# Finishing the next image's layer 0 before layer 3, outputs on another queue, and a new order for the last image's gated MLP

## The chip, the cores and the metric

The kernel runs on one core of one Trainium2 chip. The metric is device time in microseconds (us), as the median of several executions. The engines are named as in the profile: PE is TensorE (matrix multiplies), PEld its weight loads, DVE is VectorE, ACT is ScalarE, POOL is GpSimd, SP is SyncE, which here only issues DMAs.

## The reference

Four images of 192 channels by 64 x 64 positions, float32, go through four layers:

- Layer 0: LayerNorm; a 3x3 convolution gives offsets for a deformable gather (nine taps, bilinear); channel attention (six heads) with a projection, and a residual; then LayerNorm, an MLP 192 to 768 to 192 with exact GELU, and a residual.
- Layer 1: non-local attention of all 4096 positions with each other, in 96 channels (theta, phi, g), projected back, and a residual.
- Layer 2: attention in overlapping 8x8 windows, a projection, a gate made of pyramid means and a depthwise 3x3; then a gated MLP:

```python
z = gelu(fc1(layernorm(x)))           # 768 channels
z1, z2 = z[:384], z[384:]
x = x + fc2(z1 * dwconv3x3(layernorm(z2)))
```

- Layer 3: the means of an image's channels go through a small net to four weights per channel; these are the taps of a causal depthwise 3x3 (the row above and the left neighbour), plus a bias: the output.

## The kernel before

**The loop over images.** For each image b: `keys(b)` makes phi and g for all positions, `layer1(b)` runs the attention, with layer 0's gather of image b+1 woven between its steps, `windows(b)` does the window attention, and `rest(b)` does projection and gate, the gated MLP and layer 3. For b = 1 and 2, `offsets(b+1)` (LayerNorm and offset convolution of the image after next) is made chunk by chunk beside the keys. Positions are worked in eight chunks of 512 (NCH = 8).

**Layer 0's MLP of the next image.** `mlp0(b+1)` needs the gather's result only, so `rest(b)` weaves it beside its own work. It is a generator of 33 steps: one of preparation and four for each chunk i, here written i.w01, i.w23, i.w45n1, i.n0. The first three widen two blocks of 128 hidden channels each (matmuls L844 and L851, Gelu on ACT L858); the third also narrows the upper 64 channels (L870), the fourth the lower 128 (L867), adds the result (L874 on DVE), and stores the chunk to DRAM by SP's queue (L894). `keys(b+1)` loads that store again (L907, also SP) ahead of its first matmul (L910); then come g (L915), and the copies of phi by ACT (L911) and of g by DVE (L918). The last step of the last chunk ends with `keep_warm(p, 12)` (L737), matmuls whose results nobody reads.

**Credits.** The projection, the MLP and layer 3 yield amounts; `rest` adds them up, and for each whole credit runs one step of `mlp0`:

```python
for part in main():
    credit += part
    while credit >= 1.0:
        next(other, None)
        credit -= 1.0
for _ in other:
    pass
```

With the amounts before, the last three steps of `mlp0` (7.w23, 7.w45n1, 7.n0 with keep_warm) fall to layer 3's yields. In the last image (`alone`) there is no next one and `other` is empty.

**What sets the order.** Inside the gated MLP the order on each engine is the order of the program, written out by hand (`tc.manual_schedule()`), with the woven steps of `mlp0` in it. Outside it (layer 3, keys, offsets) the framework's planner orders instructions when the kernel is compiled: by readiness in its own estimate of times, ties by program order. Each engine and each DMA queue then runs its own list strictly in order.

**The gated MLP.** It works in four rounds j = 0..3, each on a pair of chunks: `widen(j, ms)` (fc1 for blocks ms, L1574 and L1576, Gelu L1580; blocks 0 to 2 are z1, 3 to 5 are z2), `gate_mean`, `gate_difference`, `gate_square`, `gate_variances`, `gate_scale` (the LayerNorm of z2: L1586, L1590, L1595, L373, L1613), and the depthwise taps of older pairs. A depthwise needs a row of the next pair, so round j does the upper taps of pair j-1 and the lower ones of pair j-2, then `narrow(j-2)` (fc2, L1659 and L1664) and `end()` (L1673, adds to x and sums its channels). After the four rounds a tail does the last two pairs, `pairs - 2` and `pairs - 1`. The taps are DVE multiply-adds (L1377); in the last image two of nine taps (five in the last pair) are matmuls by diagonals on PE (L1368), with DVE joining in at L1370. L1647 multiplies the finished gate into z1. z1, z2 and the accumulators have two buffers each; the MLP's matmuls share five PSUM banks "h".

**Layer 3.** Means (L1766 ff.), the small net (L1771, L1782, L1785), the weights w (L1789); then six units u. ACT writes the first tap (L1819), POOL a column (L1822), DVE adds the three others (L1838), and the unit is stored by one or two DMAs of SP's queue (L1840, L1844). `o` has three buffers. In the last image one unit's taps run on PE.

Of the kernel before, what the change touches and what calls it, by code (L numbers as in the profile page):

```python
# [24 lines left out]
M, Q = 128, 64  # L25
NCH = 8
# [55 lines left out]
def conv_seq_kernel(ctx: ExitStack, tc: tile.TileContext, a, out: bass.AP):  # L82
# [1459 lines left out]
    def mlp(b, x, sums, sb, ps, taps, hn):  # L1542


        with ExitStack() as s:
# [134 lines left out]
            with tc.manual_schedule():  # L1680
                in_order.append(None)
                for j in range(pairs):
                    lo, hi, upper, lower = 2 * j, 2 * j + 1, j - 1, j - 2
                    if lower >= 0:
                        lower_taps(lower, 0)
                    if upper >= 0:
                        yield 1.0
                    widen(j, (3, 4))
                    if lower >= 0:
                        lower_taps(lower, 1)  # L1690
                    yield 1.0
                    if lower >= 0:
                        lower_taps(lower, 2)
                        narrow(lower, (0, 1))
                        narrow(lower, (2,))
                    if upper >= 0:
                        upper_taps(upper, 0, 2)
                    end()
                    widen(j, (5, 0))
                    gate_mean(lo)  # L1700
                    gate_mean(hi)
                    if upper >= 0:
                        upper_taps(upper, 0)
                        upper_taps(upper, 1, 2)
                    gate_difference(lo)
                    gate_square(lo)
                    gate_difference(hi)
                    widen(j, (1,))
                    gate_square(hi)
                    widen(j, (2,))  # L1710
                    if upper >= 0:
                        upper_taps(upper, 1)
                        upper_taps(upper, 2, 2)
                    gate_variances(lo, hi)
                    norm = None
                    if j + 1 < pairs:
                        norm = pair_norm_steps(x, j + 1, sb, ps, f"l2n2_{b}_{j + 1}")
                        links(norm, SQUARE)
                    yield 1.0
                    if norm is not None:  # L1720
                        links(norm, VARIANCE)
                        table(GELU)
                    gate_scale(lo)
                    gate_scale(hi)
                    hns.pop(j)
                    if norm is not None:
                        hns[j + 1] = links(norm)
                    if upper >= 0:
                        upper_taps(upper, 2)
                for m in range(3):  # L1730
                    lower_taps(pairs - 2, m)
                    yield 1.0
                narrow(pairs - 2, (0, 1, 2))
                for m in range(3):
                    upper_taps(pairs - 1, m, 2)
                    end()
                    yield 0.5
                    upper_taps(pairs - 1, m)
                    yield 0.6
                    lower_taps(pairs - 1, m)  # L1740
                    yield 0.7
                narrow(pairs - 1, (0, 1))
                narrow(pairs - 1, (2,))
                end()
                in_order.pop()


    def layer3(b, x, sums, ps, alone):

        with ExitStack() as s:  # L1750
# [37 lines left out]
            w = s1.tile([M, 2, 4], F32, name=f"w3_{b}", tag="w")  # L1788
            nc.vector.tensor_tensor(w, pw, VW["l3_b2"][:, :, 0:4], ALU.add)  # L1789
            flat = out[b].rearrange("c h w -> c (h w)")  # L1790
            diag = None
            if alone:
                diag = s1.tile([M, 4, M], F32, tag="diag3", name=f"diag3_{b}")
# [2 lines left out]
            for u in (0, 1, 2, 4, 3, 5):  # L1796
                k = u // 4
                o = sb.tile([M, UN], F32, tag="o", name=f"out_{b}_{u}", bufs=3)
                ov = o.rearrange("p (r c) -> p r c", c=W)
                bias3 = VW["l3_bias"][:, k]  # L1800
                if alone and u == 1:
                    xv = x[:, 0 : 4 * UN].rearrange("p (r c) -> p r c", c=W)
                    for j in range(0, UR, 8):
                        at = UR * u + j
                        src, up = xv[:, at : at + 8], xv[:, at - 1 : at + 7]
                        p = ps.tile([128, CN], F32, tag="h", name=f"po3_{b}_{u}_{j}")
                        pv = p.rearrange("p (r c) -> p r c", c=W)
                        terms = [
                            (1, pv, up),
                            (0, pv[:, :, 1:W], up[:, :, 0 : W - 1]),  # L1810
                            (2, pv[:, :, 0 : W - 1], up[:, :, 1:W]),
                            (3, pv[:, :, 1:W], src[:, :, 0 : W - 1]),
                        ]
                        for n, (tap, to, of) in enumerate(terms):
                            nc.tensor.matmul(to, lhsT=diag[:, tap, :], rhs=of, start=n == 0, stop=n == 3, skip_group_check=True)
                        nc.scalar.activation(ov[:, j : j + 8], pv, AF.Identity, bias=bias3)
                else:
                    src = x[:, bass.ts(u, UN)].rearrange("p (r c) -> p r c", c=W)
                    nc.scalar.activation(  # L1819
                        ov[:, :, 1:W], src[:, :, 0 : W - 1], AF.Identity, bias=bias3, scale=w[:, k, 3:4]  # L1820
                    )
                    nc.gpsimd.tensor_copy(ov[:, :, 0:1], bias3.unsqueeze(1).to_broadcast([M, UR, 1]))  # L1822
                    if k == 0:

                        a0 = 1 if u == 0 else 0
                        xv = x[:, 0 : 4 * UN].rearrange("p (r c) -> p r c", c=W)
                        rows = [(ov[:, a0:], xv[:, UR * u - 1 + a0 : UR * u + UR - 1])]
                    else:
                        v, two = 2 * (u - 4), o.rearrange("p (k r c) -> p k r c", k=2, c=W)
                        rows = [(two[:, i, 1:8], blocks[:, v + i, 0:7]) for i in range(2)]  # L1830
                        rows.append((two[:, :, 0], over[:, v : v + 2, 0]))
                    for to, up in rows:
                        for tap, to, of in (
                            (1, to, up),
                            (0, to[..., 1:W], up[..., 0 : W - 1]),
                            (2, to[..., 0 : W - 1], up[..., 1:W]),
                        ):
                            nc.vector.scalar_tensor_tensor(to, of, w[:, k, tap : tap + 1], to, ALU.mult, ALU.add)  # L1838
                if k == 0:
                    nc.sync.dma_start(out=flat[0:M, bass.ts(u, UN)], in_=o)  # L1840
                else:
                    to = flat[M:C].rearrange("c (j h n) -> c j h n", h=2, n=CN)[:, 2 * (u - 4) : 2 * (u - 4) + 2]
                    for h in range(2):
                        nc.sync.dma_start(out=to[:, :, h], in_=o[half(h)].rearrange("p (k n) -> p k n", k=2))  # L1844
                yield 0.7

    def rest(b, x, others, oi, sums, m2):


        with ExitStack() as s:  # L1850
            alone = m2 is None
            sb = s.enter_context(pool_of(name="norms", bufs=1))
            ps = s.enter_context(pool_of(name="restps", bufs=2, space=PSUM))
            wide = s.enter_context(pool_of(name="restps2", bufs=5, space=PSUM))
            psums = Psums({"n": ps, "v": ps, "h": wide}, {"t": "h"})
            other = iter(())
            if not alone:
                other = mlp0(b + 1, m2, s.enter_context(pool_of(name="l0d", bufs=1)), sb, psums)
            credit = 0.0

            def main():
                hn = []

                def ahead():
                    hn.append(links(pair_norm_steps(x, 0, sb, psums, f"l2n2_{b}_0")))

                yield from project(b, x, others, oi.pop(), psums, HFT_PE if alone else (), ahead)
                yield from mlp(b, x, sums, sb, psums, GATE_PE if alone else (), hn)
                yield from layer3(b, x, sums, psums, alone)

            for part in main():
# [6 lines that stand above are left out]
# [170 lines left out]
```

## Time and profile before

| what | value |
|---|---|
| median of 3 runs | 6800.64 us (6798.39 to 6806.05) |
| profiled execution | 6757.88 us |
| its span | 6756.1 us |
| mean granted TensorE clock | 0.952 |
| PE busy | 6155.1 us, 91% |
| DVE busy | 4694.1 us, 69% |
| ACT busy | 3599.2 us, 53% |
| POOL busy | 2065.4 us, 31% |
| output stores on SP's queue, images 0 to 2 | 8 per image (4 of 512 KB, 4 of 256 KB) |
| rest of image 0: last product L1647 to first key matmul L910 | 2298.28 to 2335.82 us |
| last image: rounds 1, 2, 3 and tail of the gated MLP | 6482.0, 6532.7, 6601.4, 6658.1 to 6721.0 us |

The page gives the busy time of each engine in one profiled execution, and slices of the span with the busy tenths of each engine and the granted clock of PE. The timeline lists runs of instructions by start, duration, engine, line and operation, with the idle time before them in brackets and what ended it. Windows give busy times for chosen stretches. Timeline and windows share the time axis, microseconds from the start of the span. All rounds of the last image are measured at the steps of DVE: from the first upper taps of one round to those of the next.

### The profile page before, as it was taken

What the parts mean: (1) busy time and instruction counts of PE and PEld (TensorE: products, weight loads), DVE (VectorE), ACT (ScalarE), POOL (GpSimd) and SP (SyncE); (2) the same over time, 40 slices, a digit from 0 to 9 for tenths busy, and PEclk for the clock granted to TensorE, in tenths of its full rate; (3) what the DMA queues carried; (4) which work ended last, traced back from release to release, by engine and by line L of the source; (5) the groups of instructions that cost most, each with busy time, mean ns of one, the idle gap of its engine ahead of it and who ended that gap; (6) DMA issues with size and microseconds to landing.
All of it is one profiled execution on the core that took longest, in us unless ns stands there. A gap on an engine that the chain in (4) does not pass through costs nothing.

```text
span 6756.1 us, 115795 instructions
## 1 busy us (share of the span) xinstructions
PE 6155.1 (91%) x45392; PEld 4180.0 (62%) x45392; DVE 4694.1 (69%) x6908; ACT 3599.2 (53%) x6136; POOL 2065.4 (31%) x2276
## 2 busy tenths in 40 slices
PE   7687999999989899999998899999998889999986
PEld 4455578786644458887654457878664457776532
DVE  3664279985677758996576848988567867765656
ACT  3664368774444358885444338877444435544332
POOL 2654057662200027672210007765220000012200
PEclk8788999999989899999999999999999999999998
DMA  6885156661010156663110047665101010010000
GB/s 188 260 280 177 54 177 217 215 196 42 8 43 15 59 181 200 219 211 93 29 31 26 17 132 218 216 208 165 35 24 30 17 54 10 15 28 22 4 7 21
DMA packets 330496, 699.37 MB, mean 104 GB/s; under 512 B 60077, under 2 KB 217181, under 8 KB 329182
## 3 DMA queue, kind: packets, MB, share of 16 engines
q0 software_dynamic: 92736, 455.22, 21.0%
q1 hardware_dynamic: 236382, 235.95, 12.3%
q8 instruction: 358, 5.87, 0.4%
q14 instruction: 188, 1.54, 0.1%
q10 hardware_dynamic: 832, 0.79, 0.0%
HBM read 611.25 MB, written 78.87 MB: 102 GB/s over the span
## 4 chain that ended last, share of the span: by engine, by line
PE 51%; DVE 17%; ACT 4%; issue 4%; DMA 2%; SPq 0%; POOL 0%; another core or an unknown queue 0%; DVEq 0%; ACTq 0%; POOLq 0%
PE y L1031 8%; PE s L963 7%; PE h L634 3%; PE v L1196 2%; PE h L1574 2%; DVE ha L1377 2%; PE qk L1121 2%; PE qk L1122 2%; PE t L1204 1%; DVE gate L1377 1%; PE zm L1586 1%; DVE ga L1377 1%; PE h L1576 1%; PE s L1157 1%; PE rb L1270 1%
## 5 line engine op out<-in xcount | busy, mean ns | idle before, releaser
L616 POOL DMA_INDIRECT ring<-table,idx x1152 | 1634.7, 1419 | 1132.5 <-issue 217.8
L963 PE MATMUL s<-ths,ph 96*128 96x256 f32 x4096 | 991.5, 383 | 8.5 <-ACT xo L626 2.7
L963 PEld LDWEIGHTS s<-ths,ph 96*128 96x128 f32 x4096 | 784.0, 193 | 137.1 <-ACT ths L957 4.7
L622 ACT ACTIVATE row<-ring,pos 128x384 f32<-128x384 f32 x1152 | 672.0, 608 | 204.3 <-DVE xo L627 111.3
L1031 PE MATMUL y<-sc,gx 128*97 128x256 f32 x3008 | 724.7, 383 | 18.4 <-ACT yn L1037 15.1
L623 DVE SCALAR_TENSOR_TENSOR row<-ring,fr,row 128x384 f32<-128x384 f32 x1152 | 674.8, 613 | 91.6 <-ACT row L622 63.1
L1031 PEld LDWEIGHTS y<-sc,gx 128*97 128x97 f32 x3008 | 492.5, 165 | 150.8 <-ACT yn L1037 16.5
L626 ACT ACTIVATE xo<-row,pos 128x192 f32<-128x192 f32 x1152 | 485.8, 448 | 156.9 <-remote 63.8
L627 DVE SCALAR_TENSOR_TENSOR xo<-row,fr,xo 128x192 f32<-128x192 f32 x1152 | 447.1, 412 | 123.3 <-issue 60.6
L1028 DVE TENSOR_TENSOR sc<-sc,mbs 128x1024 f32<-128x1024 f32 x376 | 453.4, 1218 | 46.1 <-ACT mbs L989 26.5
L965 ACT COPY sc<-s 128x1024 f32<-128x1024 f32 x376 | 377.5, 1004 | 177.5 <-PE s L963 141.5
L970 DVE TENSOR_TENSOR top<-top,sc 128x1024 f32<-128x1024 f32 x282 | 344.5, 1222 | 137.4 <-ACT sc L965 115.9
L634 PE MATMUL h<-ti,xo 128*128 128x192 f32 x2304 | 437.1, 328 | 0.0
L1029 ACT ACTIVATE sc<-sc 128x1024 f32<-128x1024 f32 x376 | 393.4, 1053 | 75.6 <-DVE sc L1028 66.5
L634 PEld LDWEIGHTS h<-ti,xo 128*128 128x128 f32 x2304 | 390.9, 190 | 29.0 <-issue 8.6
L1180 DVE TENSOR_REDUCE es<-ex 128x6 f32<-128x384 f32 x264 | 133.3, 546 | 365.0 <-ACT ex L1176 365.0
L634 PE MATMUL h<-kept,xo 128*128 128x192 f32 x960 | 255.9, 402 | 114.1 <-DVE xo L627 61.5
L634 PEld LDWEIGHTS h<-kept,xo 128*128 128x128 f32 x960 | 183.0, 224 | 209.5 <-DVE xo L627 98.6
L1624 POOL COPY gate<-gate 128x192 f32<-128x192 f32 x12 | 4.2, 351 | 1000.4 <-ACT gate L1617 855.0
L1377 DVE SCALAR_TENSOR_TENSOR ga<-gate,v,ga 128x1024 f32<-128x1024 f32 x234 | 300.4, 1284 | 6.7
L1031 PE MATMUL y<-se,gx 128*97 128x256 f32 x1088 | 268.3, 387 | 8.6 <-ACT se L1029 8.1
L858 ACT ACTIVATE gl<-h,bias_fc 128x256 f32<-128x256 f32 x384 | 151.2, 474 | 232.9 <-PE h L851 232.5
(391 smaller groups left out, 11213.0 us busy)
## 6 DMA issues: line engine op xcount, KB each, us to landing
ti<-table SPq DMA_DIRECT2D x768, 48.0 KB
ring<-table,idx POOLq DMA_INDIRECT x1152
xnd<-xn SPq DMA_DIRECT2D x4, 3270.0 KB
xi<-in_x_dram SPq DMA_DIRECT2D x32, 384.0 KB
xk<-xd SPq DMA_DIRECT2D x32, 384.0 KB
xd<-xc SPq DMA_DIRECT2D x64, 192.0 KB
table<-tt SPq DMA_DIRECT2D x32, 384.0 KB
xc<-xd SPq DMA_DIRECT2D x60, 192.0 KB
```

Of the source, the lines that this page charges most:

```text
L616: nc.gpsimd.indirect_dma_start(out=gt.rearrange("p q r c -> p (q r c)"), out_offset=None, in_=corners, in_offset=bass.IndirectOffsetOnAxis ...
L622: nc.scalar.activation(row, gt[:, 0], AF.Copy, scale=pos[:, t, 9 + tap : 10 + tap])
L623: nc.vector.scalar_tensor_tensor(row, gt[:, 1], fr[:, t, 9 + tap : 10 + tap], row, ALU.mult, ALU.add)
L626: nc.scalar.activation(xo[:, j, :], row[:, 0, :], AF.Copy, scale=pos[:, t, tap : tap + 1])
L627: nc.vector.scalar_tensor_tensor(xo[:, j, :], row[:, 1, :], fr[:, t, tap : tap + 1], xo[:, j, :], ALU.mult, ALU.add)
L634: nc.tensor.matmul(acc[m // 2][:, bass.ts(m % 2, C)], lhsT=xo.rearrange("p j c -> p (j c)")[:, bass.ts(m, 128)], rhs=tt, start=t == 0 and ...
L963: nc.tensor.matmul(p[:, t, :], lhsT=ph[:, bass.ts(G * g + t, 128)], rhs=ths[i], start=True, stop=True)
L965: nc.scalar.copy(to, p)
L1028: nc.vector.tensor_tensor(ex, ex, mbs[i].unsqueeze(1).to_broadcast([128, G, QN]), ALU.add)
L1029: nc.scalar.activation(ex, ex, AF.Exp)
L1031: nc.tensor.matmul(py, lhsT=gx[:, G * g + t, :], rhs=ex[:, t, :], start=g == 0 and t == 0, stop=g == NG - 1 and t == G - 1,)
L1377: nc.vector.scalar_tensor_tensor(acc[:, b], src(tap, b), w[:, tap : tap + 1], acc[:, b], ALU.mult, ALU.add)
```

## The change

There are four edits.

1. In images 0 to 2 the nine yields of the MLP's tail give 0.9 each instead of 0.5, 0.6 and 0.7, and a new `yield 4.0 * NCH` ahead of layer 3 makes room for whatever of `mlp0` is left. Counted out, the tail's nine yields now run 5.n0, 6.w01, 6.w23, 6.w45n1, 6.n0, 7.w01, 7.w23, 7.w45n1 and 7.n0, one each, so that all 33 steps are done and the new yield finds none. Before, six steps (5.n0 to 7.w01) fell to the tail and three to layer 3. 7.n0 with its keep_warm comes into the MLP's hand-written order, ahead of the last `narrow`.
2. Layer 3's eight output DMAs per image are issued by POOL (`nc.gpsimd`) in images 0 to 2; the last image's stay on SP.
3. In the last image (`taps`) a round puts `widen(5, 0)`, the means, the differences and the first square ahead of `narrow(lower)`, `end()` and the upper taps, and one step of upper taps behind the next pair's squares; the tail mixes upper taps of the last pair with lower ones of the one before, and narrows block by block.
4. In images 0 to 2 the two calls `narrow(lower, (0, 1))`, `narrow(lower, (2,))` of a round become `narrow(lower, (0, 1, 2))`: the matmuls of the upper channels (L1664) of blocks 0 and 1 no longer stand ahead of those that read block 2 (L1659).

```diff
@@ gated MLP, a round j
                     if lower >= 0:
                         lower_taps(lower, 2)
-                        narrow(lower, (0, 1))
-                        narrow(lower, (2,))
-                    if upper >= 0:
-                        upper_taps(upper, 0, 2)
-                    end()
-                    widen(j, (5, 0))
-                    gate_mean(lo)
-                    gate_mean(hi)
...
+                    if taps:
+                        widen(j, (5, 0))
+                        gate_mean(lo)
+                        gate_mean(hi)
+                        gate_difference(lo)
+                        gate_square(lo)
+                        gate_difference(hi)
+                        if lower >= 0:
+                            narrow(lower, (0, 1, 2))
+                        end()
+                        widen(j, (1,))
+                        gate_square(hi)
+                        if upper >= 0:
+                            upper_taps(upper, 0, 2)
+                        widen(j, (2,))
+                        gate_variances(lo, hi)
+                        if upper >= 0:
+                            upper_taps(upper, 0)
+                            upper_taps(upper, 1, 2)
+                    else:
+                        if lower >= 0:
+                            narrow(lower, (0, 1, 2))
...
                     yield 1.0
+                    if taps and upper >= 0:
+                        upper_taps(upper, 1)
+                        upper_taps(upper, 2, 2)
@@ gated MLP, the tail
+                one, two = pairs - 2, pairs - 1
+                if taps:
+                    lower_taps(one, 0)
+                    upper_taps(two, 0)
+                    lower_taps(one, 1)
+                    upper_taps(two, 1)
+                    narrow(one, (0,))
+                    lower_taps(one, 2)
+                    narrow(one, (1,))
+                    narrow(one, (2,))
+                    upper_taps(two, 2)
                     end()
-                    yield 0.5
-                    upper_taps(pairs - 1, m)
-                    yield 0.6
-                    lower_taps(pairs - 1, m)
-                    yield 0.7
-                narrow(pairs - 1, (0, 1))
-                narrow(pairs - 1, (2,))
+                    for m in range(3):
+                        lower_taps(two, m)
+                        narrow(two, (m,))
+                else:
...
+                    for m in range(3):
+                        upper_taps(two, m, 2)
+                        end()
+                        yield 0.9
+                        upper_taps(two, m)
+                        yield 0.9
+                        lower_taps(two, m)
+                        yield 0.9
+                    narrow(two, (0, 1))
+                    narrow(two, (2,))
                 end()
@@ layer3
+            by = nc.sync if alone else nc.gpsimd
...
-                    nc.sync.dma_start(out=flat[0:M, bass.ts(u, UN)], in_=o)
+                    by.dma_start(out=flat[0:M, bass.ts(u, UN)], in_=o)
...
-                        nc.sync.dma_start(out=to[:, :, h], in_=o[half(h)].rearrange("p (k n) -> p k n", k=2))
+                        by.dma_start(out=to[:, :, h], in_=o[half(h)].rearrange("p (k n) -> p k n", k=2))
@@ rest
                 yield from mlp(b, x, sums, sb, psums, GATE_PE if alone else (), hn)
+                yield 4.0 * NCH
                 yield from layer3(b, x, sums, psums, alone)
```

More of the change, by code (lines that the diff above doesn't have):

```diff
@@ L1683, in mlp @@
                     lo, hi, upper, lower = 2 * j, 2 * j + 1, j - 1, j - 2
+                    more = j + 1 < pairs
                     if lower >= 0:
@@ L1693, in mlp @@
                         lower_taps(lower, 2)
-                        narrow(lower, (0, 1))
-                        narrow(lower, (2,))
-                    if upper >= 0:
-                        upper_taps(upper, 0, 2)
-                    end()
-                    widen(j, (5, 0))
-                    gate_mean(lo)
-                    gate_mean(hi)
[L1702 to L1714, printed above, removed]
+                    if taps:
[20 more added lines that the diff above has]
+                            narrow(lower, (0, 1, 2))
+                        if upper >= 0:
+                            upper_taps(upper, 0, 2)
+                        end()
+                        widen(j, (5, 0))
+                        gate_mean(lo)
+                        gate_mean(hi)
+                        if upper >= 0:
+                            upper_taps(upper, 0)
+                            upper_taps(upper, 1, 2)
+                        gate_difference(lo)
+                        gate_square(lo)
+                        gate_difference(hi)
+                        widen(j, (1,))
+                        gate_square(hi)
+                        widen(j, (2,))
+                        if upper >= 0:
+                            upper_taps(upper, 1)
+                            upper_taps(upper, 2, 2)
+                        gate_variances(lo, hi)
@@ L1715, in mlp @@
                     norm = None
-                    if j + 1 < pairs:
+                    if more:
                         norm = pair_norm_steps(x, j + 1, sb, ps, f"l2n2_{b}_{j + 1}")
@@ L1719, in mlp @@
                     yield 1.0
-                    if norm is not None:
+                    if taps and upper >= 0:
+                        upper_taps(upper, 1)
+                        upper_taps(upper, 2, 2)
+                    if more:
                         links(norm, VARIANCE)
@@ L1725, in mlp @@
                     hns.pop(j)
-                    if norm is not None:
+                    if more:
                         hns[j + 1] = links(norm)
@@ L1729, in mlp @@
                         upper_taps(upper, 2)
[L1730 to L1735, printed above, removed]
-                    end()
-                    yield 0.5
-                    upper_taps(pairs - 1, m)
-                    yield 0.6
-                    lower_taps(pairs - 1, m)
-                    yield 0.7
-                narrow(pairs - 1, (0, 1))
-                narrow(pairs - 1, (2,))
+                one, two = pairs - 2, pairs - 1
[9 more added lines that the diff above has]
+                    upper_taps(two, 2)
+                    end()
+                    for m in range(3):
[3 more added lines that the diff above has]
+                    for m in range(3):
+                        lower_taps(one, m)
+                        yield 1.0
+                    narrow(one, (0, 1, 2))
+                    for m in range(3):
+                        upper_taps(two, m, 2)
+                        end()
+                        yield 0.9
[5 more added lines that the diff above has]
+                    narrow(two, (2,))
                 end()
```

## The prediction

> **What bounds the kernel now.** I read the page's slices first, then the transition from image 0 to image 1 in the timeline and in windows, then the same for the other images, and last the gated MLP of the last image. TensorE (PE) is busy 91% of the span and its chain holds 51% of it, so time is to be had only where PE idles or runs at a lower clock. The slices show where:
>
> ```profile
> PE   7687999999989899999998899999998889999986
> PEclk8788999999989899999999999999999999999998
> ```
>
> A slice is 169 us. PE is full while keys and scores run, and at 8 or less near the rests (the windows, MLP and layer 3 of an image), and at the very end. All three edits lie there. The timeline of the first transition (start, duration, engine, line, operation; in brackets the idle before and its releaser):
>
> ```profile
> 2298.28 1.28 DVE L1647 SCALAR_TENSOR_TENSOR z<-gate,v,z 128x1024 f32<-128x1024 f32 x1
> 2307.35 0.17 DVE L1789 TENSOR_TENSOR w<-pw,wide 128x8 f32<-128x8 f32 x1 [2.35 <-PE pw L1785]
> 2307.24 3.78 PE L844 MATMUL h<-d_l0m,fc 128*128 128x256 f32 x8
> ...
> 2308.88 9.50 DVE L1838 SCALAR_TENSOR_TENSOR out<-x,w,out 128x960 f32<-128x960 f32 x8 [1.36 <-ACT out L1819]
> ...
> 2316.04 2.81 PE L870 MATMUL o<-gl,fc 128*64 128x256 f32 x24
> ...
> 2318.78 5.42 PE L867 MATMUL o<-gl,fc 128*128 128x512 f32 x12
> ...
> 2325.55 8.01 PE L737 MATMUL o<-bias,ident 128*128 128x384 f32 x24 [1.36 <-DVE xa L874]
> ...
> 2335.82 2.54 PE L910 MATMUL tp<-xk,phiT 96*96 96x512 f32 x4 [2.26 <-DMA xk<-xd]
> ```
>
> Layer 3 can start at w (2307.35). While VectorE (DVE) works it off, PE does what is left of layer 0's MLP of the next image: widen (L844), narrow (L870, L867) and 8 us of keep_warm (L737). The keys follow only at 2335.8, since they read that MLP's output back. Windows by stage (length, busy time of PE, PEld, DVE, ACT, POOL, granted clock, DMA share, GB/s):
>
> ```profile
> 2243.00:2303.50 60.50, 52.63 (x214) 27.24 (x210) 48.73 (x59) 13.65 (x26) 1.92 (x14) 0.94 0.08 24
> 2303.50:2336.00 32.50, 27.63 (x121) 16.85 (x122) 25.30 (x39) 11.44 (x15) 11.62 (x15) 0.89 0.41 127
> 2336.00:2390.00 54.00, 53.46 (x295) 33.42 (x295) 17.89 (x24) 17.70 (x26) 0.00 (x0) 0.84 0.34 96
> ...
> 2340.00:2344.00 4.00, 4.00 (x12) 2.36 (x11) 0.56 (x1) 0.00 (x0) 0.00 (x0) 0.50 0.26 73
> ```
>
> PE idles 7.9 us in the MLP's tail and 4.9 in layer 3, and then the keys run at half clock: the windows of 4 us from 2336 to 2356 have 0.63, 0.50, 0.50, 0.50 and 0.73. That is 4 x (0.37+0.5+0.5+0.5+0.27) = 8.6 us lost, at a full engine. Image 1 has the same (0.84 over 3926 to 3980); image 2 has not, its gap ahead of the keys is 1.46 us.
>
> **Part 1: layer 0's MLP ends ahead of layer 3.** By the credits, the tail's nine yields now give a step each, and the last three steps leave layer 3. Useful PE work moved per image: two widens of two blocks (8 x L844 1.9 + 8 x L851 1.1 = 3.0 each, 6.0), narrow(1) 2.8, narrow(0) 5.4: 14.2 us. With them go 8.0 us of keep_warm, two L874 sums on DVE (0.48 + 0.75), four Gelus each of two widens on ACT (1.57 each four) and three xd stores on SP, which stand nowhere near their limits. The tail has 7.9 us of PE idle, but in bits beside DVE's taps (48.7 of 60.5 us busy), so the last z multiply comes later by between 14.2 - 7.9 - 5.4 = 1 us (narrow(0) stands behind it and delays no tap) and 14.2 - 7.9 = 6.3; I take 4: it ends at 2303.6 instead of 2299.6. Then the hand order bites: inside the MLP PE keeps the order written, so keep_warm (8.0) and what it waits for (L874, 0.75) stand ahead of the last narrow. That takes 3.7 + 1.9 + 2.0 + 1.1 = 8.7 us: 2303.6 + 0.75 + 8.0 + 8.7 = 2321, then end() 1.5, the means and the small net 4, so w comes about 2326, 18 us later than 2307.4. Layer 3's 25 us of DVE end near 2352 instead of 2334.
>
> Against that: the keys' PE need not wait for layer 3. Their input was stored before keep_warm ended, so they start near 2321 instead of 2335.8, 14.8 us earlier, with no gap ahead and so up to 8.6 us of clock. What is late next is DVE: each of the keys' eight chunks needs a gx copy (0.56), and in images 1 and 2 the LayerNorm for offsets 3.45 us more (1.22 + 0.95 + 1.28), while layer 3's multiplies are ahead of them by priority. PSUM has two banks for the keys, so some three chunks (3 x 3.75 = 11 us of PE) go before PE depends on DVE. If the copies slip into DVE's gaps, the transition gains 15 + 8.6 = 23; if they wait for 2352, PE idles 20 us and the clock falls anew: 15 - 20 + 8.6 - 8.6 - (4 from the tail) = -9, call it -14 with the LayerNorm behind. Layer 3's tiles and multiplies wait for ACT and POOL again and again (1.36, 0.55, 0.36 us in the rows), and the order outside the MLP is made by readiness, so I take the middle, +7 per transition, and 6 for image 2 (no clock to win, no offsets to wait for): **-20 us** of time, bounds +42 and -60.
>
> The Trainium skill, "TensorE: Matmul & The Clock Gate", section "What's actually happening", has the clock fall after an idle window of some 3.4 us and return after some 3.4 us of sustained work. The row disagrees with both: the gap was 2.3 us and the low clock held for 17 us. By the page a gap of 2.3 us costs nothing, and part 1 would win no clock here, -12 instead of -20.
>
> **Part 2: outputs from GpSimd's queue.** Eight issues per image leave SP (L1840, L1844; 0.33 to 0.65 us each), where the loads of xk stood behind L1840's wait for DVE: out at 2330.23, xk at 2330.74. So the earlier keys of part 1 depend on it. On POOL a direct load (L1070) takes 0.65 to 0.71 us; 8 x 0.68 = 5.4 us in a stage where POOL is busy 11.6 of 32.5. Behind these waiting issues stand POOL's copies (L1822) of the next unit and the offsets' constants (L483, L484). A copy that waits behind an output's issue would delay ACT's start of a unit by at most one issue, 0.7 us; 6 units at 0 to 0.7 are 0 to 4 us per image, and three out tiles give room. I take 0, since the start of layer 3's first unit has no output ahead of it, and its price is in the +7's lower bound.
>
> The Trainium skill, "SBUF — State Buffer", section "Who interferes with whom", speaks against this part: a DMA issued from GpSimd can stall because GpSimd is starved of its port by DVE, and should go to another queue. By the page a DVE operation with two SBUF inputs, as layer 3's multiplies, holds up only GpSimd operations that read SBUF; taken at its worst, each of eight issues waits for one multiply (1.28 us), 10 us per image on POOL. No row before shows such a stall.
>
> **Part 3: the last image's rounds.** There is no next image, and two taps of nine run on PE. One round of four:
>
> ```profile
> 6552.13 1.98 PE L1659 MATMUL f<-z,fc2T 128*128 128x512 f32 x4 [1.31 <-DVE z L1647]
> ...
> 6557.18 0.75 DVE L1370 SCALAR_TENSOR_TENSOR ga<-gate,v,gt 128x512 f32<-128x512 f32 x1 [5.10 <-PE gt L1368]
> ...
> 6558.60 3.91 PE L1574 MATMUL h<-d_l2n,fc1T 128*128 128x512 f32 x8
> ```
>
> PE waits for DVE's z, narrows, and only then serves the taps and widen; DVE waits 5.1 us for the taps, later 6.1 (behind the means, L1586) and 5.6 (behind pb_z), 23 us in the round. The new order puts widen, means (5.4 us of PE) and differences ahead of that narrow. Rounds as DVE steps through them last 50.7, 68.7 and 56.7 us (6482 to 6658), with PE busy 45.8, 55.9 and 45.5. Laying the same instructions in the new order with the durations of the rows gives 46.2, 55.4 and 48.4, that is PE's own time: 26 us less. The price: Gelu of z1's first block of round j now waits for narrow of j-2 (two buffers), some 8 us after before's place, but ACT is busy only 20 of 69 us. The tail (6658 to 6721, 62.9) I get at 63 to 66: five PE taps per block (9.0 us) and narrow (8.3) fill PE either way. So **-23 us**, bounds -10 (DVE still waits behind the means, 6 in each round, and the tail at +3) and -32 (DVE's 44.9, 39.7 and 24.6 bind).
>
> **Part 4, small:** in images 0 to 2 narrow (0,1) and (2) of a lower pair become one call. PE loses 1.9 us of L1664 that filled the wait for the last z. The waits there are short, 0.5 us ahead of L1659 in the rows above; six such calls at 0 to 1.7: 0 to 10 us, near the lower end, **+2**.
>
> **Sum.** -20 - 23 + 2 = -41 on the profiled execution's 6757.9 (span 6756.1 and 1.8 around it): 6717. The median of the runs is 6800.6, 42.8 above; I carry this difference over whole: **6760 us**.
>
> **Rivals.** (A) Slower: keep_warm and the last narrow delay w by 18 us, and DVE does all of layer 3 before the keys' copies. It decides once more than some 15 of layer 3's 25 us on DVE stand ahead of the copies of the third chunk. For it: layer 3 comes first in the program. Against: its bubbles. 3 x 14 - 23 = +19 with nothing for part 4: 6820. (B) The last image gains next to nothing, as the tail eats it: -20 + 2: 6783. (C) Copies slip in, the clock stays full: 3 x 20 + 23 = -83 with part 4 hidden: 6718. (D) The change does not do what it says at the transitions: PE's early keys only wait longer for DVE, net 0, -23 + 2: 6780.
>
> **Chances.** Forecast 0.50 (its own range 6745 to 6775), C 0.13, B and D together 0.25, A 0.12. About 0.2% (14 us) is what can be told from no change here. Faster: 0.50 + 0.13 + half of B and D = 0.76; same: 0.12, the other half; slower: A, 0.12. The range leaves out A and the end of C: 6722 to 6795.
>
> **What would show it.** Part 1: no gap ahead of the first L910, and clock 1.0 there; keep_warm between the last two L1659 groups; w 18 us after its old place; wrong if L910 starts but PE then waits for L918's copies. Part 2: output issues on POOL, xk loads ahead of layer 3's outputs. Part 3: L1590 ahead of L1370 in a round, rounds near 46, 55 and 48, tail near 63. The forecast fails most likely in the order of DVE between layer 3 and the keys.

## The result, and the profile after

The kernel after takes 6841.4 us (median of 14 runs, 6821.3 to 6860.6) against 6800.6 for the kernel before (14 runs beside them): ratio 1.006, 95% interval 1.0042 to 1.0077. It is about 41 us slower, where the prediction said 41 us faster. Its profiled execution has a span of 6838.6 us and a mean granted clock of 0.946.

The slices of the page of after, to be laid beside those of before:

```profile
PE   7777999999988899999998889999998889999997
PEclk8789989999999989999999989999999999999998
```

They look alike: the dips near the rests are as wide as they were. Stretches whose instructions didn't change differ by up to 24 us from one profile to another (the scores of one image), so I compare stage by stage, from marks that both traces have. The rows below are image 0's rest and what follows it (after, timeline; layer 3's weights w are now at L1829, its multiplies at L1879, the small net's matmuls at L1811 to L1825):

```profile
2341.19 1.28 DVE L1647 SCALAR_TENSOR_TENSOR z<-gate,v,z 128x1024 f32<-128x1024 f32 x1
2343.19 8.01 PE L737 MATMUL o<-bias,ident 128*128 128x384 f32 x24 [2.62 <-DVE xa L874]
2351.04 3.60 PE L1659 MATMUL f<-z,fc2T 128*128 128x512 f32 x8
2359.36 1.96 PE L910 MATMUL tp<-xk,phiT 96*96 96x512 f32 x4
2366.39 0.88 PE L1825 MATMUL pw<-t,w2T 48*64 48x1 f32 x16
2367.32 0.17 DVE L1829 TENSOR_TENSOR w<-pw,wide 128x8 f32<-128x8 f32 x1 [2.13 <-PE pw L1825]
...
2394.35 2.02 PE L910 MATMUL tp<-xk,phiT 96*96 96x512 f32 x2 [6.69 <-DVE gx L918]
```

The order is the one foretold: keep_warm (L737) and the last narrow (L1659) stand ahead of everything, the weights come 24.8 us after the last z ends instead of 7.8, and the keys (L910) start before them, 16.9 us after that z instead of 36.2. New is the last row: PE waits 6.7 us for a copy of g. Windows of the same stretch (length; busy PE, PEld, DVE, ACT, POOL; granted clock; DMA share; GB/s):

```profile
2342.50:2369.10 26.60, 25.91 (x117) 14.34 (x118) 4.68 (x16) 2.95 (x4) 2.43 (x16) 1.00 0.28 76
2369.10:2396.00 26.90, 18.13 (x84) 10.80 (x83) 25.38 (x35) 8.21 (x9) 10.04 (x20) 0.82 0.62 201
2396.00:2430.00 34.00, 28.88 (x143) 16.48 (x141) 9.23 (x11) 8.32 (x14) 1.15 (x2) 0.64 0.14 40
```

PE is full and at full clock until the weights are there; then it idles beside layer 3's 25.4 us on DVE, and behind that it runs at 0.64. Taken apart over a whole transition, from the last z to the first scores (idle: no matmul on PE; clock: half of PE's busy time at half clock; rest: the work at full clock):

| stage | kernel | us | idle | clock | rest |
|---|---|---|---|---|---|
| fc1 to last z, image 0 | before | 308.1 | 34.1 | 8.0 | 266.0 |
| | after | 315.1 | 35.1 | 6.0 | 274.0 |
| | part 1 alone | 311.3 | 31.0 | 6.1 | 274.2 |
| last z to scores, 0 to 1 | before | 159.5 | 11.2 | 12.9 | 135.4 |
| | after | 166.3 | 22.3 | 17.1 | 126.9 |
| | part 1 alone | 172.2 | 15.7 | 30.6 | 125.9 |
| 1 to 2 | before | 157.8 | 10.1 | 12.3 | 135.4 |
| | after | 169.0 | 21.2 | 21.0 | 126.8 |
| 2 to 3 | before | 66.5 | 5.7 | 4.9 | 55.9 |
| | after | 71.8 | 9.0 | 14.6 | 48.1 |

The work is the same: 8 us of it went ahead of the last z. But with part 1 alone it filled only 3 of the 34 us of idle time there (4 and 5 in the next two images), and behind it idle time and low clock grew by more than the 8 us that left.

The last image did what was forecast. From its first fc1 matmul to its last product, before and after (windows, then DVE's wait for the taps on PE, before and after, from the lists of waits with us, times and longest):

```profile
6436.70:6717.20 280.50, 226.92 (x813) 96.50 (x811) 167.68 (x163) 82.50 (x116) 12.32 (x24) 0.91 0.01 1
```

```profile
6547.00:6800.10 253.10, 219.56 (x813) 94.26 (x811) 168.30 (x163) 82.83 (x116) 12.32 (x24) 0.95 0.01 1
```

```profile
DVE ga L1370 <- PE gt L1368: 56.6, 14, 11.1
DVE ga L1370 <- PE gt L1368: 24.3, 14, 4.2
```

It is 27.4 us shorter. DVE's wait for the taps fell by 32 us; PE's own busy time fell by 7 us with the clock, 0.95 instead of 0.91.

### The profile page after: what moved, and what is told of

It is laid out like the page before. It is cut to its first block, busy times and chain, and to the rows that moved or that the text cites. A ratio compares the mean times of both kernels' runs of the same rounds, so it can differ in the third digit from the quotient of the medians.

```text
span 6838.6 us, 115793 instructions
## 1 busy us (share of the span) xinstructions
PE 6197.0 (91%) x45392; PEld 4200.5 (61%) x45392; DVE 4694.9 (69%) x6908; ACT 3591.2 (53%) x6131; POOL 2068.7 (30%) x2300
## 4 chain that ended last, share of the span: by engine, by line
PE 39%; DVE 14%; ACT 3%; issue 3%; DMA 1%; POOL 1%; another core or an unknown queue 0%; SPq 0%; DVEq 0%; ACTq 0%; POOLq 0%
PE y L1031 7%; PE s L963 6%; PE h L634 2%; PE v L1196 2%; PE h L1574 1%; DVE ha L1377 1%; PE qk L1121 1%; DVE row L623 1%; PE qk L1122 1%; DVE top L970 1%; PE t L1204 1%; DVE gate L1377 1%; PE s L1157 1%; PE rb L1270 1%; DVE sc L1028 1%
## 5 line engine op out<-in xcount | busy, mean ns | idle before, releaser
L963 PE MATMUL s<-ths,ph 96*128 96x256 f32 x4096 | 999.3, 386 | 8.7 <-issue 4.8
L963 PEld LDWEIGHTS s<-ths,ph 96*128 96x128 f32 x4096 | 790.9, 194 | 139.4 <-issue 5.6
L1031 PE MATMUL y<-se,gx 128*97 128x256 f32 x1088 | 266.0, 385 | 4.9 <-ACT se L1029 4.3
```

Source lines behind the costliest of these rows:

```text
L963: nc.tensor.matmul(p[:, t, :], lhsT=ph[:, bass.ts(G * g + t, 128)], rhs=ths[i], start=True, stop=True)
L1031: nc.tensor.matmul(py, lhsT=gx[:, G * g + t, :], rhs=ex[:, t, :], start=g == 0 and t == 0, stop=g == NG - 1 and t == G - 1,)
```

## The experiments

The kernel before ran again beside each group of runs (medians 6768.7, 6755.7, 6786.1 and 6779.6 us), so across groups only the ratios to it compare. "So many us better than after" is a difference of two ratios, uncertain by some 16 to 19 us.

**The four parts, each alone on the kernel before.**

> The kernel before with part 1 alone: 0.9 at the nine yields of the tail and the yield of 4.0 * NCH ahead of layer 3; outputs stay on SP's queue. Theory A (part 1 delays layer 3: keep_warm and the last narrow stand ahead of its weights, then the copies of g wait behind layer 3's multiplies, PE idles some 7 us and runs some 30 us at half clock): slower, by 12 to 20 us in each of three transitions, 36 to 60 in all; w some 25 us after the last z instead of 8. Theory B (part 1 itself gains, GpSimd's queue loses it): 10 to 30 us faster than before.

```diff
-                    yield 0.5
+                    yield 0.9
...
+                yield 4.0 * NCH
                 yield from layer3(b, x, sums, psums, alone)
```

6816.5 us against 6768.7: ratio 1.0075 (1.0049 to 1.0102), 48 us slower. Theory A's sign and size hold, B falls. The weights come 24.8, 26.5 and 26.5 us after the last z, the keys 16.9, 18.6 and 18.6, so they start early without part 2 as well. Summed over the two stages of the table and the three images, against the mean of the two profiles of before (the second stands below), the work at full clock is 2 us less, the idle time 5 us more and the clock takes 48 us more. So what part 1 costs is nearly all clock.

> The kernel before with part 2 alone: layer 3's outputs of images 0 to 2 from GpSimd's queue. Theory A: within 5 us of before per transition, and if anything faster by some 2 us in each, since the loads of xk no longer wait behind the outputs on SP; the first key matmul some 2 us nearer to the end of keep_warm. Theory B: slower by 10 us or more in each transition, as GpSimd's copies and constants wait behind the issues: 30 to 60 in all.

```diff
-                    nc.sync.dma_start(out=flat[0:M, bass.ts(u, UN)], in_=o)
+                    by.dma_start(out=flat[0:M, bass.ts(u, UN)], in_=o)
```

6769.4 against 6768.7: 1.0006 (0.9986 to 1.0025). In its profile the gap ahead of the first key matmul is gone (first transition) and no low clock falls into the keys, yet PE waits longer for the last sum of layer 0's MLP (4.9 instead of 1.4 us, L874 on DVE):

```profile
2349.95 10.34 PE L737 MATMUL o<-bias,ident 128*128 128x384 f32 x24 [4.87 <-DVE xa L874]
```

The gain is below what can be told.

> The kernel before with part 3 alone, the new order of the last image's gated MLP. Both theories: 27 us faster than before (the profiles of the two kernels give 280.5 us from the first fc1 matmul to the last product before, 253.1 after); images 0 to 2 unchanged.

Its edit is part 3 of the diff. 6734.7 against 6768.7: 0.995 (0.9926 to 0.9974), 34 us faster, 27.4 of them in the MLP of the last image (253.1 us). As expected.

> The kernel before with part 4 alone: one narrow of three blocks in the rounds of images 0 to 2. Both theories: 0 to 10 us slower, that is 0 to 1.7 at each of six places; 2 expected, and less than can be told from no change.

```diff
-                        narrow(lower, (0, 1))
-                        narrow(lower, (2,))
+                        narrow(lower, (0, 1, 2))
```

6796.6 against 6768.7: 1.0037 (1.0012 to 1.0062). The MLP stage is 2.9 to 3.5 us longer in each of three images, 9.5 in all; the interval of the time, 8 to 42 us, just holds it. The place, before:

```profile
2184.14 1.28 DVE L1647 SCALAR_TENSOR_TENSOR z<-gate,v,z 128x1024 f32<-128x1024 f32 x1
2185.48 1.98 PE L1659 MATMUL f<-z,fc2T 128*128 128x512 f32 x4 [0.27 <-DVE z L1647]
...
2188.41 3.70 PE L1574 MATMUL h<-d_l2n,fc1T 128*128 128x512 f32 x8
```

and with part 4 alone:

```profile
2215.76 1.28 DVE L1647 SCALAR_TENSOR_TENSOR z<-gate,v,z 128x1024 f32<-128x1024 f32 x1
2217.11 2.67 PE L1659 MATMUL f<-z,fc2T 128*128 128x512 f32 x4 [2.14 <-DVE z L1647]
2219.71 3.75 PE L1664 MATMUL f<-z,fc2T 128*64 128x512 f32 x12
...
2223.39 3.70 PE L1574 MATMUL h<-d_l2n,fc1T 128*128 128x512 f32 x8
```

PE now stands idle for the 1.9 us in which it had done L1664, and does it behind the last z: the next fc1 (L1574) starts 7.6 us after that z begins instead of 4.3.

**What in part 1 costs: pieces taken out of after.**

> The kernel after with keep_warm left out of the rests (the 24 matmuls whose results nobody reads; it stays ahead of image 0's keys). Theory A1 (the 8 us of keep_warm in the hand-written order carry through to layer 3's weights and to the keys): the weights come 17 us after the last z instead of 25, and each of three transitions from the last z to the first scores (166, 169 and 72 us in the profile of after) is 8 us shorter: 24 us faster than after, still some 15 slower than before. Theory A2 (keep_warm holds the clock up; without it the keys start at half clock): 0 to 8 us longer each.

```diff
-            if i == NCH - 1:
+            if i == NCH - 1 and b == 0:
                 keep_warm(p[:, 0:384], 12)
```

1.001 of before (0.9988 to 1.0033), where after is at 1.006: some 34 us better; by the uncertainty above, the 24 of A1 lies within. The run takes away 24 us of work as well as its place in the order, and the same was not tried on the kernel before, so what the place alone costs is not shown by it. Weights 15.4, 21.0 and 16.4 us after the last z. In image 1 of its profile the clock took 45.8 us, so A2's danger is real, but not the rule.

> The kernel after with the copies of g (L918) on ScalarE instead of VectorE, so that they can't stand behind layer 3's multiplies; the order on PE is the same instruction by instruction. Theory A3 (PE's idle time between the keys' chunks, 6.7 us ahead of L910, and the 30 us at half clock behind it come from these copies): the idle goes, and the first two transitions are 7 to 20 us shorter, the third 5: 20 to 45 us faster than after. Rival (the copies only hide the next wait, the LayerNorm of the offsets on VectorE or its loads): less than 10 us in all, and the half clock stays, some 10 us later or earlier.

```diff
-            nc.vector.tensor_copy(gx[:, bass.ts(i, 4), 0:P], p)
+            nc.scalar.copy(gx[:, bass.ts(i, 4), 0:P], p)
```

1.0053 (1.0035 to 1.0072): next to nothing, as the rival had it. My theory A3 falls: PE's idle time between the keys did go, but the transitions stay at 169.9, 169.8 and 71.1 us, because the clock takes what the idle time gave back. The windows show how (first transition):

```profile
2340.30:2343.70 3.40, 3.40 (x40) 3.37 (x39) 0.20 (x2) 2.05 (x3) 0.45 (x1) 0.99 0.32 96
2343.70:2379.00 35.30, 35.30 (x106) 23.59 (x105) 23.25 (x30) 11.63 (x16) 10.51 (x21) 0.50 0.57 167
```

PE does not idle at all in either, and still the clock halves at 2343.7. What PE did in the 3.4 us before is the small net, 24 matmuls of a single column (1.9 us), and part of a key chunk:

```profile
2340.23 1.05 PE L1822 MATMUL pw<-t,w2T 48*128 48x1 f32 x8
2341.21 0.88 PE L1825 MATMUL pw<-t,w2T 48*64 48x1 f32 x16
```

And a full engine of key matmuls for 35 us does not bring the clock back. From this came theory A4.

> The kernel after without the ninth credit in the tail: the last step of the next image's MLP (narrow of the lower channels, stores, keep_warm) is run by the new yield behind the gated MLP, outside its hand-written order. Theory A (the hand-written order is what delays layer 3): the last narrow of the gated MLP comes straight after its last z; the weights come some 8 to 20 us after it instead of 25, layer 3 ends as much earlier, and each transition is 5 to 15 us shorter than in after: 15 to 45 us in all. Rival (the planner puts keep_warm ahead of the small net all the same): the weights at 20 to 25 us, under 5 us shorter each.

```diff
                         lower_taps(two, m)
-                        yield 0.9
+                        if m < 2:
+                            yield 0.9
```

1.0033 (1.0012 to 1.0053), some 18 us better than after: the lower end of what theory A gave. Its rows:

```profile
2312.86 1.98 PE L1659 MATMUL f<-z,fc2T 128*128 128x512 f32 x4 [0.75 <-DVE z L1647]
...
2321.19 8.01 PE L737 MATMUL o<-bias,ident 128*128 128x384 f32 x24 [0.58 <-DVE t L1817]
2330.92 1.96 PE L910 MATMUL tp<-xk,phiT 96*96 96x512 f32 x4
2331.02 0.17 DVE L1830 TENSOR_TENSOR w<-pw,wide 128x8 f32<-128x8 f32 x1 [9.29 <-PE pw L1826]
```

The narrow follows the last z at once, but the planner puts keep_warm between the small net's two layers: the weights still come at 18.2 us.

**Theory A4: the clock falls for matmuls that move little, and the keys don't lift it.**

> The kernel before with part 2 (its keys follow on keep_warm with no gap, and run at full clock) and 32 added matmuls with one column each ahead of the first key matmul of images 1 to 3, some 3 us in which PE counts as busy in the profile; their result is overwritten. Theory A4 (a stretch of matmuls that move next to nothing halves the clock as idling does, and the keys' own matmuls don't lift it again): the clock is 0.5 from the first key chunk until the LayerNorm means (L394) join in, or to the end of the keys in image 3; the transitions 3 us longer for the added work and 6 to 20 for the clock, 30 to 55 slower than part 2 alone in all. Rival (only idle time halves it): the clock stays 1.0, 6 to 12 us slower in all.

```diff
+            if i == 0 and b > 0:
+                for _ in range(32):
+                    nc.tensor.matmul(p[:, 0:1], lhsT=phiT[:, 0, :], rhs=x[:, 0, 0:1], start=True, stop=True)
```

1.0098 (1.0072 to 1.0124), about 62 us above part 2 alone, more than the 55 expected. The keys of image 3 in its profile:

```profile
5590.20:5658.40 68.20, 67.64 (x214) 47.60 (x214) 4.46 (x8) 6.95 (x10) 0.02 (x1) 0.50 0.15 43
```

and those of image 3 with part 2 alone, without the added matmuls:

```profile
5513.00:5551.00 38.00, 36.69 (x188) 24.64 (x188) 13.67 (x24) 7.02 (x10) 3.38 (x7) 1.00 0.47 140
```

The same keys, PE as full, take about twice the time at half clock, to their last matmul and on into the first scores: 54 of the 68 us are keys, the rest added matmuls ahead of them and theta and scores behind. In images 1 and 2 the clock was low for 37.5 us; it didn't come back with the LayerNorm's first means (L394), which ran within it, but 15 us behind them.

So the first half of A4 is shown: one-column matmuls bring the half clock with no wait of PE. The second half is no rule. In the first profile of after the clock came back among the keys alone in all three transitions, after 3.4, 10.2 and 10.2 us at half, each time at the end of a group of phi matmuls (L910). In the first one these take 3.51 us, and the next ones 1.88:

```profile
2369.07 3.51 PE L910 MATMUL tp<-xk,phiT 96*96 96x512 f32 x4
...
2374.24 1.88 PE L910 MATMUL tp<-xk,phiT 96*96 96x512 f32 x4
```

The wait of 6.7 us for g then halved it again.

> The kernel after with the 24 matmuls of keep_warm moved from the end of the next image's MLP to behind the small net of layer 3 (L1822, L1825), in images 0 to 2. Theory A4 (the small net's one-column matmuls halve the clock, which the keys don't lift): the half clock ahead of the keys goes; what is lost by the clock between the last z and the first scores falls from 15 to 21 us to under 8 in the third transition at least; the weights 15 to 18 us after the last z instead of 25; each transition 10 to 16 us shorter than in after. Rival (the clock falls by PE's idle time behind the wait for the copies of g alone): the low clock begins behind that wait as in after, and each transition is 0 to 5 us shorter.

```diff
-            if i == NCH - 1:
+            if i == NCH - 1 and b == 0:
...
+            if not alone:
+                keep_warm(ps.tile([128, CN], F32, tag="h", name=f"warm3_{b}")[:, 0:384], 12)
             w = s1.tile([M, 2, 4], F32, name=f"w3_{b}", tag="w")
```

1.0024 (1.0003 to 1.0044): some 24 us better than after, no better than leaving keep_warm out. The weights come at 15.6 to 15.8 us and the small net no longer halves the clock; but a gap of 3.5 us between two key chunks does, for 30.7 us (first transition). Small matmuls and gaps both act: either cause is enough.

**Is there a version in which part 1 pays?**

> The kernel before with parts 2 and 3, without parts 1 and 4: the parts that alone measured no change and 34 us faster. All theories: 27 to 35 us faster than before; by the gap that part 2 closed ahead of the first key matmul another 0 to 10.

Parts 2 and 3 of the diff. 6720.6 against 6755.7: 0.9948 (0.9928 to 0.9968), 35 us faster than before, no different from part 3 alone (0.995).

> A mended part 1 on top of parts 2 and 3, without part 4: the last step of the next image's MLP is left to the new yield, outside the hand-written order; no keep_warm in the rests; copies of g on ScalarE. Theory A4: layer 3's weights 8 to 12 us after the last z, as before; but the small net halves the clock and the keys run at 0.5 for 30 to 55 us: transitions of 145 to 155, 145 to 155 and 50 to 58 us against 151, 152 and 65 in the kernel with parts 2 and 3, whose tails are 3 us shorter each: within 15 us of that kernel, 25 to 45 faster than before. Rival (order and copies were all): no low clock, transitions near 130, 130 and 42, 60 to 75 us faster than before.

Besides the edits of a_last_step_out and a_gx_on_scalar, no keep_warm in the rests, and part 4 undone. 1.0022 (1.0007 to 1.0037): weights at 10.9 us, transitions 166.3, 152.6 and 70.3, with 30.9, 18.5 and 28.3 us lost to the clock. Slower than expected: layer 3 is no longer late, yet nothing is won.

> The same as c_mended_no_warm with 12 of the 24 matmuls of keep_warm (4 us) behind layer 3's small net. Theory A4: the clock is lifted ahead of the keys and stays; transitions near 135, 135 and 46 us: 15 to 30 us faster than c_mended_no_warm, 55 to 75 faster than before. Rival: 12 us slower than c_mended_no_warm, three times 4 us.

0.9988 (0.9965 to 1.0011); it didn't keep the clock. Its rows show where it falls:

```profile
2357.30 6.73 PE L737 MATMUL warm<-bias,ident 128*128 128x384 f32 x12
...
2369.06 1.92 PE L915 MATMUL g<-gT,xk 96*128 96x96 f32 x16
...
2372.96 3.70 PE L910 MATMUL tp<-xk,phiT 96*96 96x512 f32 x4 [1.98 <-DMA xk<-xd]
```

A wait of 2 us for the keys' input, and L910 runs at half speed from there, for 54.6 us.

> c_mended_warm with four buffers for the keys' input in every image instead of two in images 1 and 2. If the gaps of 2 to 3 us between the keys' chunks come from the two buffers (theory): no such gap, no low clock in the keys of images 1 and 2, those transitions near 140 us instead of 169, 50 us faster than c_mended_warm. If they come from the loads themselves, as image 3 with its four buffers and a gap of 2.1 us suggests: the gaps and 55 us at half clock stay, within 10 us.

```diff
-                    b, ph, gx, s2.enter_context(pool_of(name="l1k", bufs=2 if 0 < b < B - 1 else 4)),
+                    b, ph, gx, s2.enter_context(pool_of(name="l1k", bufs=4)),
```

0.9993 (0.9972 to 1.0014), transitions 155.1, 166.4 and 65.3: gaps of 1.5 and 3.6 us stay, and 20 to 29 us of clock. So the buffers don't decide the time. All three hold part 3's gain, and are still some 50, 27 and 30 us slower than parts 2 and 3 without part 1: no version of part 1 here pays.

**Chance and size.**

> The kernel before, unchanged, for a second profile. If stages with the same instructions differ between kernels only by chance, the score stages of this profile (first scores to last, 666, 677, 670 and 464 us in the first one) lie within 10 to 25 us of them either way, and the stretch from the last z to the first scores is 150 to 160, 150 to 160 and 62 to 67 us.

Score stages of 668, 676, 673 and 464 us, transitions 149.7, 157.5 and 66.5. In the first of them the gap ahead of the keys was 2.0 us, but the clock didn't fall there: 2.7 us lost instead of 12.9.

> The kernel after, unchanged, for a second profile. If its long score stages in the first profile (682, 683 and 693 us against 666, 677 and 670 before) are chance, they are nearer to 670 here; if they belong to the change, they are above 680 again. The stages that the change touches repeat within 5 us: 314 to 316 us from the first fc1 matmul to the last z, then 166, 169 and 72 to the first scores.

314.4, 314.4 and 313.2 us to the last z; transitions 174.1, 174.0 and 69.1, with 31 us of clock in the first two, now straight behind the small net. Score stages 670, 688, 679 and 466.

> The kernel after with part 4 undone (parts 1, 2 and 3 stay). The profile of part 4 alone had its MLP stage 3 us longer per image, its measured time 28 us. If the stage is all: 10 us faster than after, 25 to 35 slower than before. If part 4 costs what was measured: 28 faster than after, 10 to 15 slower than before.

1.0031 (1.0016 to 1.0046), some 20 us better than after; both sizes lie within what it can tell. The MLP stages of images 0 to 2 are some 10 us shorter in all.

## Why the prediction was wrong

**Part 1, the step that failed: "I take the middle, +7 per transition".** The two steps ahead of it were right: the last z 4 us later (it was 1 to 3 with part 1 alone), the weights 18 us later (20 with part 1 alone: 3 with the last z and 17 behind it), the keys from 17 us behind the last z (16.9). The step failed on "with no gap ahead and so up to 8.6 us of clock": I counted the half clock of before as something that a gap ahead of the keys causes and an early start removes. The runs show that the keys, once the clock is halved, can run on at it for up to 54 us, and that they now start beside the small net and beside layer 3, where one-column matmuls and waits for copies and loads halve it: 10 to 31 us lost per transition instead of 3 to 13. In before they started late, behind keep_warm, with no small net among them; where the clock fell into them there, it came back after 17.1 us. So an early start of 19 us was worth less than nothing: with part 1 alone the transitions are 18, 18 and 9 us longer than the mean of before's two profiles, 44 us in all, and the stages ahead of them 7 us; measured were 48, where -20 was taken.

**Rival A** had the sign and nearly the price (14 per transition; 16 with part 1 alone), the price by luck: it stood on 20 us of idle time each, where idle time grew by 6 us behind the last z and the clock's loss by 18. Its copies behind layer 3's multiplies are there (6.7 us) but do not decide: with the copies on ScalarE the time stayed. Keep_warm in the hand order, its other half, has its share: 34 us better without it, 18 with the last step out of that order, and how much of either is its place is open.

**Part 2**: 0 taken, 0 measured; but "the earlier keys of part 1 depend on it" is wrong, as they start as early with part 1 alone. **Part 3**: -23 taken, -27.4 in the stage, right in mechanism and size. By rounds, from fc1 to fc1 (the new order moves the taps, the prediction's marks): 44.4, 50.0, 68.7 and 117.5 with the tail before, 43.5, 46.6, 56.3 and 106.7 after. **Part 4** is a mis-sized term: +2 taken, near 10 in the stages, the upper end of my bounds, and 28 in time (8 to 42). I read the wait of 0.5 us as what it costs, and that one stands in the tail (ahead of L1659 at 2299.62; none of the rows that I showed has it). In the round above the wait was 0.27 us because PE had done 1.9 us of L1664 in it; that work is what counts.

**The sum.** Measured alone the four parts give 48 + 1 - 34 + 28 = 43 us, against 41 for the whole, so what was taken wrong is parts 1 and 4. In the stages: 53 us in the three rests and transitions (means of two profiles each), less 27 in the last image, 25 in all; measured 41, interval 28 to 52. Another part lies in the score stages of images 1 to 3, whose instructions didn't change: 1824 us in the mean of the 11 profiles of kernels that have part 1, 1811 in the six without it and without added matmuls, so some 14 more. Why they are longer is not shown, and with single profiles that differ by 10 us I call it open. Open too is what sets the clock: shown is only behind which matmuls and gaps it fell here, and that among the keys it sometimes came back and sometimes didn't.

The page of the Trainium skill that the prediction weighed ("TensorE: Matmul & The Clock Gate", "What's actually happening") lets sustained work lift the clock after some 3.4 us. For the scores (L963) the runs come near it: where they began at half clock, it came back 3.7 to 7.1 us later. For the keys they don't agree: 54 us of them at 0.50, in a window of 68.2 us with PE busy for 67.6.

## What to carry to other kernels

Moving work ahead of a stage helps only if it fills idle time there; here 8 us of it filled 3 to 5 of some 35. A hand-written order also carries along whatever is tied to the moved step (keep_warm) and sets it ahead of what others wait for. Before starting a stage earlier, look at what it will then stand beside, and read the granted clock next to the busy time: a full PE is no proof of full speed. Small changes in several places are best predicted, and measured, one by one: here one part cost nothing, one gained 34 us, and two lost 76 together.

## What the hardware showed unexpectedly

- The clock halved with no idle time at all, behind 3.4 us that held 1.9 us of one-column matmuls, and stayed at 0.50 for 35 us and more of uninterrupted key matmuls (in other places it came back among them after 3.4 or 10.2 us); added one-column matmuls alone brought 37.5, 37.5 and 68.3 us of it.
- The low clock is not the same from run to run: in the first transition of before a gap of 2.3 us ahead of the keys was followed by 17.1 us at half clock in one profile, a gap of 2.0 us by none in the other.
- Eight output DMAs issued by GpSimd instead of SyncE (0.53 to 0.64 us each on POOL) cost nothing that can be measured.
